# Attention's matmuls as four 64x64 products at a time, and the values of two groups over two steps

## Chip, cores and metric

The kernel runs on one core of one Trainium2 chip, in one launch. The metric is the device time of that launch in microseconds; lower is better.

## What is computed

The input is 8 images of 512 channels by 32x32 pixels (N = 1024 pixels), all in float32. Two attention blocks follow each other. Cut to what matters here:

```python
# layer 0: group norm, 8 heads of 64 channels, projection, group norm, residual
hn  = group_norm(x, gn1_scale, gn1_bias)
qkv = einsum('bchw,oc->bohw', hn, w_qkv) + b_qkv          # 1x1 convolution
q, k, v = split(qkv.reshape(b * 8, 3 * 64, n), 3, axis=1)
wgt = softmax(einsum('bct,bcs->bts', q * 64**-0.25, k * 64**-0.25))
a   = einsum('bts,bcs->bct', wgt, v)
x   = x + group_norm(einsum('bchw,oc->bohw', a, w_proj) + b_proj, gn2_scale, gn2_bias)
# layer 1: one head of 512 channels with weight norm and RMS norm
qkv = einsum('oc,bcn->bon', weight_norm(v_qkv, g_qkv), x)
qkv = qkv / (rms(qkv) + 1e-4)
h   = einsum('bij,bcj->bci', softmax(q^T k * 512**-0.5), v)
x   = (x + einsum('oc,bcn->bon', weight_norm(v_out, g_out), h)) * 2**-0.5
```

The change concerns layer 0's attention: the projections of q and k, the scores (q times k) and the values (softmax times v).

## The kernel before

**Order.** Every engine call goes through `InOrder` (line 26), which pins it to the order in which the Python code makes it. What an engine does next is therefore written out by hand, and each engine works its list strictly in that order. A float32 matmul of the program stands in the trace as two MATMULs and two LDWEIGHTS (weight loads), two passes over the same tile.

**Layer 0's attention.** For each image `b`, the loop at line 1414 runs 32 steps (`STEPS`). A step `i = 8j + r` treats 128 query pixels (block `r` of 8) of a pair of heads (`j` of 4): the pair's 128 channels lie on the 128 partitions, one head on each half. `Heads.step` (line 635) issues in this order:

1. `softmax(i)`, line 573: for each of the two heads DVE takes the negated row maximum of the scores (`nm<-s`, 128x1024) and ACT the exponential with the row sum (`p<-s,nm`).
2. `values(g)`, line 610, where it is due: TensorE multiplies v by the transposed softmax `pT` of a group `g` of two steps (`RG` = 2, so 256 query pixels). There are 8 blocks of 128 key pixels and 2 heads; a matmul has 128 rows, 64 columns and 256 moving columns. The two heads' results go to the two partition halves of one PSUM bank (`po`), so two matmuls run beside each other on the two column halves of the array. ACT then adds a bias and writes `a`.
3. `fill`: a piece of a projection, where it is due.
4. `scores(i + 1)`, line 558: four matmuls of 64 rows (one head's channels), 128 columns and 512 moving columns, two at a time on the two row halves of the array, into two PSUM tiles `s` of two banks each. There are three such tiles (`ps_s`, line 102).
5. `turn()`, line 585: DVE transposes step `i - 1`'s softmax in 32x32 blocks (`pb<-p`), and SP issues four DMAs of 256 KB (`pT<-pb`) that bring it into `pT` with the key pixels on the partitions.
6. `scale()`, line 603: DVE's reciprocal of the row sums, and GpSimd (POOL) multiplies step `i`'s softmax by it.
7. `later`: GpSimd additions that a projection left over, among others.

`values(g)` comes in steps 5, 7, 9 and so on (`LAG` = 5 and `RG` = 2, lines 367 to 370); the last row of group `g` was turned in step `2g + 2`, so the step of use is the third after it. A projection piece comes in nearly every other step (`projects`, line 1421). Groups 14 and 15 come after the loop.

**Projections.** For the first image, and for each image's first pair of heads, `project_rows` (line 398) makes q and k in four pieces. A piece is 8 matmuls of 64x128 with 512 moving columns: the two row halves of the channels run beside each other into two banks, which ACT copies out and GpSimd adds. For the other pairs, `project_seven` (line 476) makes q and k from seven products instead of eight. Its first piece (n = 0) is one product of 128x128 with two terms into one bank; pieces 1 to 3 are two 64x128 products beside each other, with four terms each. At the first step of pairs 1 and 2 the short first piece is filled up with the first two key blocks of a group's values (line 1434; `values` with `most` = 2).

**Buffers.** `ps_m` (line 103) has two PSUM banks of 128x512 floats, given out in turn by `bank()` to projections and values alike. `prob` and `block`, for `p` and `pb`, have two buffers each. `pT` is taken from seven large tiles (`Slots`, line 37) that it shares with the images and v; a group's tile is given back once its values are done.

**Around it.** After an image's 32 steps come layer 0's output projection and layer 1, both made of 128x128 matmuls, with the next image's v between them. In steps 0 to 2 of the next image the last products of layer 1 (128x128) are still part of `fill`.

Of the kernel before, what the change touches and what calls it, by code (L numbers as in the profile page):

```python
# [13 lines left out]
P = 128  # L14
# [38 lines left out]
def attention_blocks_kernel(  # L53
# [133 lines left out]
    for g in range(P // SQ):  # L187
        VE.tensor_copy(same[:, g * SQ : (g + 1) * SQ], flat)
    VE.tensor_scalar_mul(same2, same, 2.0 ** 0.5)
    shift = const.tile([P, 1], F32, name="shift")  # L190
    VE.memset(shift, -16.0)
    cols = const.tile([P, NCOLS], F32, name="cols")
# [283 lines left out]
    def project_seven(b, j, right, made):  # L476

        w, tmp = near["qk7"][:, (j - 1) % 2], [near["v#"][:, k * HN : (k + 1) * HN] for k in range(3)]  # L480

        def turned(t):
            return t.rearrange("p (m be) -> p be m", be=4)

        def add(to, a, b_):
            return lambda: PO.tensor_add(to, a, b_)

        def pieces():
            pm = bank(f"pq7_{b}_{j}_0")
# [8 lines left out]
            adds = (  # L498
                ([], []),
                ([], []),  # L500
                ([add(q2, q2, q1), add(k2, k2, turned(q2))], [add(k1, k1, k2), add(k2, k2, turned(tmp[1]))]),
                ([add(q1, q1, tmp[0]), add(q2, q2, tmp[1])], [add(q2, q2, tmp[2])]),
            )
            for n in range(1, 4):
                pms = [bank(f"pq7_{b}_{j}_{n}_{r}") for r in range(2)]
                for k in range(CI):
                    for r in range(2):
                        PE.matmul(pms[r], w[halves[r], CI * n - 2 + k, :], right(r, n, k), start=(k == 0), stop=(k == CI - 1))
                if n == 1:
                    AC.activation(q1, pms[0], AF.Identity, bias=bqs[:, j : j + 1])  # L510
                    AC.copy(k1, turned(pms[1]))
                elif n == 2:
# [39 lines left out]
    class Heads:  # L552
        def __init__(self, b, hn, v, qk):
            self.b, self.hn, self.v, self.a = b, hn, v, None
            self.qk = {0: qk}
            self.pT, self.ps, self.waiting, self.open = {}, None, None, None

        def scores(self, i):
            j, r = divmod(i, NB)
            qk = self.qk[j]  # L560
            self.ps = [ps_s.tile([P, N], F32, tag="sc", name=f"s0_{self.b}_{i}_{hh}") for hh in range(2)]
            for c in range(2):
                cs = slice(c * HN, (c + 1) * HN)
                for hh in range(2):
                    PE.matmul(
                        self.ps[hh][:, cs],
                        qk[halves[hh], 0, r * P : (r + 1) * P],
                        qk[halves[hh], 1, cs],
                        start=True,
                        stop=True,  # L570
                    )

        def softmax(self, i):
            p = prob.tile([P, 4, 2, N // 4], F32, tag="p", name=f"p0_{self.b}_{i}")
# [35 lines left out]
        def values(self, g, most=NT):  # L610

            j, t0 = g // (NB // RG), g % (NB // RG) * TG
            po, s0 = self.open or (bank(f"po0_{self.b}_{g}", TG), 0)
            s1 = min(s0 + most, NT)
            self.open = (po, s1) if s1 < NT else None
            if self.a is None:
                self.a = big(f"a_{self.b}")
            for s in range(s0, s1):
                for hh in range(2):
                    ch = (2 * j + hh) * D  # L620
                    PE.matmul(
                        po[halves[hh], :],
                        self.v[:, s, ch : ch + D],
                        self.pT[g][:, :, :, hh, s, :],
                        start=(s == 0),
                        stop=(s == NT - 1),
                    )
            if self.open:
                return
# [3 lines left out]
            del self.pT[g]  # L633

        def step(self, i, fill=(), early=(), later=()):
# [12 lines left out]
            self.scale()  # L648
            for f in later:
                f()  # L650
# [763 lines left out]
    for b in range(B):  # L1414
        hn, more = heads.hn, b + 1 < B
        todo, due, rest = iter(()), [], []
        for i in range(STEPS):
            j, r = divmod(i, NB)
            due = rest

            projects = (i - LAG) % RG if not b or i not in (2, 3) else i == 3

            def project():
                nonlocal due, rest
# [27 lines left out]
            if not b:  # L1452


                if i == CI:
                    hn_next = big(f"hn_{b + 1}")
                    norm1 = Norm1(b + 1, hn_next)
                if 0 <= i - CI < CI:
                    later.append(lambda: load_x(b + 1, hn_next, i - CI))
                if 0 <= i - CI - 2 < 2 * CI:  # L1460
                    later.append(lambda: norm1.stats((i - CI - 2) // 2, i % 2))
                k = i - 3 * CI - 2
                if k == 0:
                    coeffs = norm1.gn.all_steps()
                    early += [norm1.aggregate, lambda: next(coeffs)]
                elif 0 < k < 8:
                    early.append(lambda: next(coeffs, None))
                if 0 <= k - 7 < CI // 2:
                    for ci in range(2):
                        later.append(lambda ci=ci: norm1.apply(2 * (k - 7) + ci, PO))  # L1470

            if b and j == 1 and r < 7:
                fetch_qk(CI - 1, b, slice(2 * r, 2 * r + 2))
# [143 lines left out]
```

## Time and profile before

| | |
|---|---|
| median of 3 runs | 3155.25 us (3152.35 to 3157.02) |
| the profiled execution's own time | 3153.42 us |
| its span in the profile | 3151.6 us |
| PE (matmul) busy | 3122.2 us, 99%, 13014 MATMULs |
| DVE / ACT / POOL busy | 75% / 34% / 45% |
| granted TensorE clock | 0.998 |
| DMA | 451.58 MB, mean 143 GB/s |

The profile is one execution, taken by the hardware. A row of the costliest groups reads: line, engine, operation, output tile, input tiles, shape (for matmuls: rows*columns of the array that are used, then partitions x moving columns), count, then the busy time of the group and the mean duration of one. Nearly all calls stand under line 34, the helper of `InOrder`, so groups are told apart by their tiles: `s` scores, `po` values, `pq` and `pqk` the projections by `project_seven` and `project_rows`. A timeline row gives the start, the time from the first start to the last end, and how many equal instructions were merged into it. Matmuls overlap in the pipeline, so the pitch of two is read from their starts and not from their durations.

### The profile page before, as it was taken

How to read it: one execution, taken by the hardware profiler on the slowest of the kernel's cores; microseconds unless marked ns; L12 is line 12 of the kernel's file. 1: busy time of each engine (PE TensorE's matmuls, PEld its weight loads, DVE VectorE, ACT ScalarE, POOL GpSimd, SP SyncE). 2: the span in 40 equal slices, each digit the busy share in tenths (PEclk: the TensorE clock that was granted, in tenths of full speed). 3: DMA queues.
4: the chain of work that ended last, by engine and by line, in shares of the span. 5: the costliest groups of instructions: out<-in, count | busy, mean ns of one | idle time of the engine just before them, and what ended most of it. 6: DMA issues, size and time to landing. Idle time of an engine off the chain costs nothing.

```text
span 3151.6 us, 36676 instructions
## 1 busy us (share of the span) xinstructions
PE 3122.2 (99%) x13014; PEld 1603.9 (51%) x13014; DVE 2366.5 (75%) x3213; ACT 1070.7 (34%) x1844; POOL 1409.9 (45%) x1129
## 2 busy tenths in 40 slices
PE   9999999999999999999999999999999999999899
PEld 5445554456444554445544555445554455444454
DVE  5697777867788767886679876797677877778765
ACT  2353133521245212551125502354123531245311
POOL 1555235732367314771247703566235642356114
PEclk9999999999999999999999999999999999999999
DMA  6788225862268512784128832388224872158600
GB/s 207 198 210 236 77 57 136 223 203 76 64 173 225 184 58 62 206 229 159 47 77 223 228 120 54 110 223 223 94 72 117 217 232 77 30 147 221 199 7 34
DMA packets 213950, 451.58 MB, mean 143 GB/s; under 512 B 23652, under 2 KB 42760, under 8 KB 208008
## 3 DMA queue, kind: packets, MB, share of 16 engines
q1 hardware_dynamic: 213648, 449.21, 50.3%
q8 instruction: 104, 1.70, 0.2%
q14 instruction: 78, 0.64, 0.1%
q10 hardware_dynamic: 120, 0.02, 0.0%
HBM read 137.26 MB, written 29.56 MB: 53 GB/s over the span
## 4 chain that ended last, share of the span: by engine, by line
PE 89%; DMA 3%; DVE 3%; POOL 2%; SPq 2%; issue 1%; ACT 0%; DVEq 0%; ACTq 0%; POOLq 0%
PE s L34 13%; PE po L34 12%; PE p L34 7%; PE pq L34 7%; PE p_v_T L34 6%; PE p_v_B L34 5%; PE py L34 4%; PE pqk L34 4%; PE p_u_T L34 4%; PE pa L34 4%; PE pe_e L34 3%; PE pe_bc L34 3%; PE pe_a L34 3%; PE p_o_T L34 3%; PE p_u_B L34 3%; PE p_o_B L34 2%
## 5 line engine op out<-in xcount | busy, mean ns | idle before, releaser
L34 ACT ACTIVATE p<-s,nm 128x1024 f32<-128x1024 f32 x512 | 565.6, 1109 | 794.1 <-DVE nm L34 510.2
L34 POOL TENSOR_SCALAR p<-p,tt 128x1024 f32<-128x1024 f32 x512 | 566.0, 1118 | 410.7 <-DVE tt L34 393.0
L34 DVE TENSOR_REDUCE nm<-s 128x1 f32<-128x1024 f32 x512 | 602.8, 1219 | 150.1 <-PE s L34 149.3
L34 DVE STREAM_TRANSPOSE pb<-p 128x2048 f32<-128x2048 f32 x256 | 589.9, 2304 | 37.6 <-POOL p L34 18.4
L34 PE MATMUL s<-qk 64*128 64x512 f32 x2048 | 501.5, 605 | 3.8 <-ACT p L34 2.1
L34 PE MATMUL po<-pT,v 128*64 128x256 f32 x4096 | 473.4, 383 | 1.1 <-issue 1.1
L34 PEld LDWEIGHTS po<-pT,v 128*64 128x64 f32 x4096 | 282.3, 137 | 227.9 <-issue 28.2
L34 PEld LDWEIGHTS s<-qk 64*128 64x128 f32 x2048 | 187.8, 186 | 245.7 <-issue 219.3
L34 PE MATMUL p<-e,v 128*128 128x512 f32 (+1 forms) x520 | 228.2, 590 | 2.5 <-DVE x L34 2.5
L34 POOL TENSOR_TENSOR x<-x,o 128x1024 f32<-128x1024 f32 x21 | 52.1, 2515 | 348.8 <-ACT o L34 348.8
L34 POOL TENSOR_TENSOR esum<-esum,e 128x512 f32<-128x512 f32 x96 | 141.7, 1500 | 148.4 <-ACT e L34 148.4
L34 POOL TENSOR_TENSOR u<-u,xy 128x512 f32<-128x512 f32 x64 | 79.2, 1269 | 278.0 <-DMA xy<-far_rinv 205.4
L34 PE MATMUL pq<-hn,qk 64*128 64x512 f32 (+1 forms) x420 | 191.8, 593 | 0.0
L34 ACT ACTIVATE e<-e,shift,rinv 128x512 f32<-128x512 f32 x96 | 75.8, 810 | 268.8 <-DVE e L34 268.8
L34 DVE TENSOR_TENSOR v<-v,p_v_T 128x256 f32<-128x256 f32 x300 | 114.3, 417 | 69.0 <-PE p_v_T L34 50.0
L34 PEld LDWEIGHTS p<-e,v 128*128 128x128 f32 x520 | 97.0, 190 | 130.1 <-issue 121.3
L34 PE MATMUL pqk<-hn,qk 64*128 64x512 f32 (+1 forms) x672 | 158.2, 590 | 0.0
L34 PE MATMUL pq<-t,qk 64*128 64x512 f32 x336 | 151.0, 589 | 0.0
L34 PE MATMUL pq<-v,qk 64*128 64x512 f32 x336 | 150.9, 589 | 0.0
L34 POOL TENSOR_TENSOR esum<-e 128x512 f32<-128x512 f32 x16 | 25.1, 1585 | 274.3 <-ACT e L34 274.3
L34 PE MATMUL py<-x,gram 128*128 128x512 f32 x320 | 140.6, 599 | 4.4 <-DVE x L34 4.4
L34 POOL TENSOR_TENSOR qk<-qk,v 128x512 f32<-128x512 f32 x96 | 127.2, 1335 | 3.2 <-ACT v L34 1.6
(240 smaller groups left out, 4738.1 us busy)
## 6 DMA issues: line engine op xcount, KB each, us to landing
pT<-pb SPq DMA_DIRECT2D x1024, 256.0 KB, 4.5
hn<-in_x_dram SPq DMA_DIRECT2D x32, 512.0 KB, 5.8
x<-in_x_dram SPq DMA_DIRECT2D x32, 512.0 KB, 6.9
out_dram<-x SPq DMA_DIRECT2D x63, 256.0 KB, 2.0
score<-far_score SPq DMA_DIRECT2D x8, 1792.0 KB, 7.0
value<-far_value SPq DMA_DIRECT2D x8, 1792.0 KB
v<-far_v SPq DMA_DIRECT2D x49, 256.0 KB, 4.6
proj<-far_proj SPq DMA_DIRECT2D x7, 1792.0 KB
```

What stands on the lines that cost most here:

```text
L34: return lambda *args, **kw: self._pin(call(*args, **kw))
```

## The change

All matmuls of `scores`, `project_rows` and `project_seven` become 64x64: a helper `quads` splits the 128 output columns of each into two halves, so that four matmuls, one in each quarter of the array, form a unit. The two row halves still go to two banks.

The values of two groups, `g` and `g + 1`, are made together over two consecutive steps, as 64x64 matmuls too. In the first step the upper row half (64 of each block's 128 key pixels) works for `g` in one bank and the lower half for `g + 1` in another. In the second step (`second` = 1) the halves change banks, and each bank gets the rest of its sum. Between the two, ACT copies one column of each bank into a small tile `begun`. Each bank is copied out once, at the end.

In `project_seven`, the product n = 0 is split between the first two pieces: each of them holds half of the columns of n = 1 (four terms) and half of n = 0 (two terms), both with 256 moving columns. ACT copies out four halves instead of whole banks, and GpSimd adds the row halves of n = 0.

The order changes with it. `LAG` becomes 6; values come in steps 6, 7, 10, 11, and so on to 30, 31, projection pieces in the two steps between them (8, 9, 12, 13, ...); in steps 0 to 5 they come at 0, 3, 4, 5 (for the first image 0, 2, 4, 5). The extra `values(..., 2)` at the first step of a pair is gone. The norm of the second image moves by a few steps. Groups 14 and 15 keep the old form.

```diff
-    STEPS, LAG = CI * NB, 5
+    STEPS, LAG = CI * NB, 6
+    def quads(outs, left, right, first=True, last=True):
+        for out_, l, r in zip(outs, left, right):
+            for cs in halves:
+                PE.matmul(out_[cs], l[:, cs], r, start=first, stop=last)
...
 # project_rows
                     for ci in range(CI):
-                        for r in range(2):
-                            PE.matmul(
-                                pms[r],
-                                w[halves[r], ci, :],
-                                hn[halves[r], ci, hs],
-                                start=(ci == 0),
-                                stop=(ci == CI - 1),
-                            )
+                        quads(pms, [w[rs, ci, :] for rs in halves], [hn[rs, ci, hs] for rs in halves], ci == 0, ci == CI - 1)
...
 # project_seven
-            pm = bank(f"pq7_{b}_{j}_0")
-            run(matmuls(pm, [(w[:, k, :], right(None, 0, k)) for k in range(2)]))
-            AC.copy(tmp[1], pm)
-            yield [], []
...
+            low, high = slice(0, TG), slice(TG, HN)
+            for n, cols in enumerate((low, high)):
                 pms = [bank(f"pq7_{b}_{j}_{n}_{r}") for r in range(2)]
+                product(pms, 1, cols, low)
+                product(pms, 0, cols, high)
+                AC.activation(q1[:, cols], pms[0][:, low], AF.Identity, bias=bqs[:, j : j + 1])
+                AC.copy(tmp[1][:, cols], pms[0][:, high])
+                AC.copy(k1[:, :, n * D : (n + 1) * D], turned(pms[1][:, low]))
+                AC.copy(q2[:, cols], pms[1][:, high])
+                yield [add(tmp[1][:, cols], tmp[1][:, cols], q2[:, cols])], []
+            for n in range(2, 4):
+                pms = [bank(f"pq7_{b}_{j}_{n}_{r}") for r in range(2)]
+                product(pms, n, slice(0, HN), slice(0, HN))
...
 # scores
-                for hh in range(2):
-                    PE.matmul(
-                        self.ps[hh][:, cs],
-                        qk[halves[hh], 0, r * P : (r + 1) * P],
-                        qk[halves[hh], 1, cs],
-                        start=True,
-                        stop=True,
-                    )
+                quads(
+                    [ps[:, cs] for ps in self.ps],
+                    [qk[rs, 0, r * P : (r + 1) * P] for rs in halves],
+                    [qk[rs, 1, cs] for rs in halves],
+                )
...
+        def values_two(self, g, second):
+            if not second:
+                self.pos = [bank(f"po0_{self.b}_{g + k}", TG) for k in range(2)]
+            for s in range(NT):
+                for r, rs in enumerate(halves):
+                    k = r ^ second
+                    for hh in range(2):
+                        PE.matmul(
+                            self.pos[k][halves[hh], :], self.v[rs, s, self.channels(g, hh)], self.pT[g + k][rs, :, :, hh, s, :],
+                            start=not second and s == 0, stop=s == NT - 1, skip_group_check=bool(second),
+                        )
+            for k in range(2):
+                if not second:
+                    AC.copy(begun[:, k : k + 1], self.pos[k][:, :1])
+                else:
+                    self.out(g + k, self.pos[k])
...
 # step
-            if i >= LAG and (i - LAG) % RG == 0:
-                self.values((i - LAG) // RG)
+            if i >= LAG and (i - LAG) % (2 * RG) < 2:
+                self.values_two((i - LAG) // (2 * RG) * 2, (i - LAG) % 2)
...
 # loop over the steps
-            projects = (i - LAG) % RG if not b or i not in (2, 3) else i == 3
+            projects = i in (0, 3 if b else 2, 4, 5) if i < NB else (i - LAG) % (2 * RG) > 1
...
-            if b and r == 0 and 0 < j < CI - 1:
-                fill.append(lambda: heads.values((i + 1 - LAG) // RG, 2))
```

More of the change, by code (lines that the diff above doesn't have):

```diff
@@ L189, in attention_blocks_kernel @@
     VE.tensor_scalar_mul(same2, same, 2.0 ** 0.5)
+    begun = const.tile([P, 2], F32, name="begun")
     shift = const.tile([P, 1], F32, name="shift")
@@ L497, in pieces @@
             k1, k2 = (kp[:, :, th * P : (th + 1) * P] for th in range(2))
[L498 to L502, printed above, removed]
-            )
-            for n in range(1, 4):
-                pms = [bank(f"pq7_{b}_{j}_{n}_{r}") for r in range(2)]
[L506 to L512, printed above, removed]
+            adds = {
+                2: ([add(q2, q2, q1), add(k2, k2, turned(q2))], [add(k1, k1, k2), add(k2, k2, turned(tmp[1]))]),
+                3: ([add(q1, q1, tmp[0]), add(q2, q2, tmp[1])], [add(q2, q2, tmp[2])]),
+            }
@@ new lines, in product @@
+            def product(pms, n, cols, to):
+                count = CI if n else 2
+                for k in range(count):
+                    quads(
+                        [pm[:, to] for pm in pms],
+                        [w[rs, max(CI * n - 2, 0) + k, :] for rs in halves],
+                        [(right(r, n, k) if n else right(None, 0, k)[rs])[:, cols] for r, rs in enumerate(halves)],
+                        k == 0,
+                        k == count - 1,
+                    )
+            low, high = slice(0, TG), slice(TG, HN)
@@ L514, in pieces @@
+            for n in range(2, 4):
+                pms = [bank(f"pq7_{b}_{j}_{n}_{r}") for r in range(2)]
+                product(pms, n, slice(0, HN), slice(0, HN))
+                if n == 2:
                     AC.copy(q2, pms[0])
@@ L555, in __init__ @@
             self.qk = {0: qk}
-            self.pT, self.ps, self.waiting, self.open = {}, None, None, None
+            self.pT, self.ps, self.waiting = {}, None, None
         def scores(self, i):
@@ L563, in scores @@
                 cs = slice(c * HN, (c + 1) * HN)
-                for hh in range(2):
-                    PE.matmul(
-                        self.ps[hh][:, cs],
-                        qk[halves[hh], 0, r * P : (r + 1) * P],
-                        qk[halves[hh], 1, cs],
-                        start=True,
-                        stop=True,
-                    )
+                quads(
+                    [ps[:, cs] for ps in self.ps],
+                    [qk[rs, 0, r * P : (r + 1) * P] for rs in halves],
+                    [qk[rs, 1, cs] for rs in halves],
+                )
         def softmax(self, i):
@@ L608, in scale, with out @@
             self.waiting = (i, p)
-        def values(self, g, most=NT):
+        def out(self, g, po):
             j, t0 = g // (NB // RG), g % (NB // RG) * TG
-            po, s0 = self.open or (bank(f"po0_{self.b}_{g}", TG), 0)
-            s1 = min(s0 + most, NT)
-            self.open = (po, s1) if s1 < NT else None
             if self.a is None:
                 self.a = big(f"a_{self.b}")
[L618 to L629, printed above, removed]
             AC.activation(self.a[:, j, t0 : t0 + TG], po, AF.Identity, bias=col(BV, j))
@@ L633, in values, with channels @@
             del self.pT[g]
+        def channels(self, g, hh):
+            ch = (2 * (g // (NB // RG)) + hh) * D
+            return slice(ch, ch + D)
+        def values(self, g):
+            po = bank(f"po0_{self.b}_{g}", TG)
+            for s in range(NT):
+                for hh in range(2):
+                    PE.matmul(
+                        po[halves[hh], :], self.v[:, s, self.channels(g, hh)], self.pT[g][:, :, :, hh, s, :],
+                        start=(s == 0), stop=(s == NT - 1),
+                    )
+            self.out(g, po)
+        def values_two(self, g, second):
+            if not second:
+                self.pos = [bank(f"po0_{self.b}_{g + k}", TG) for k in range(2)]
+            for s in range(NT):
+                for r, rs in enumerate(halves):
+                    k = r ^ second
+                    for hh in range(2):
+                        PE.matmul(
+                            self.pos[k][halves[hh], :], self.v[rs, s, self.channels(g, hh)], self.pT[g + k][rs, :, :, hh, s, :],
+                            start=not second and s == 0, stop=s == NT - 1, skip_group_check=bool(second),
+                        )
+            for k in range(2):
[3 more added lines that the diff above has]
+                    self.out(g + k, self.pos[k])
         def step(self, i, fill=(), early=(), later=()):
             self.softmax(i)
-            if i >= LAG and (i - LAG) % RG == 0:
-                self.values((i - LAG) // RG)
+            if i >= LAG and (i - LAG) % (2 * RG) < 2:
+                self.values_two((i - LAG) // (2 * RG) * 2, (i - LAG) % 2)
             for f in fill:
@@ L1461, in attention_blocks_kernel @@
                     later.append(lambda: norm1.stats((i - CI - 2) // 2, i % 2))
-                k = i - 3 * CI - 2
+                k = i - 4 * CI
                 if k == 0:
                     coeffs = norm1.gn.all_steps()
[L1465 to L1468, printed above, removed]
+                    early.append(norm1.aggregate)
+                if 0 <= k < 6:
+                    early += [lambda: next(coeffs, None)] * (2 if k < 2 else 1)
+                if 0 <= k - 6 < CI // 2:
                     for ci in range(2):
-                        later.append(lambda ci=ci: norm1.apply(2 * (k - 7) + ci, PO))
+                        later.append(lambda ci=ci: norm1.apply(2 * (k - 6) + ci, PO))
             if b and j == 1 and r < 7:
```

## The prediction

> **What bounds the kernel now.** The page comes first: TensorE is busy for 99% of the span, so a gain has to come out of its time.
>
> ```profile
> span 3151.6 us, 36676 instructions
> PE 3122.2 (99%) x13014; PEld 1603.9 (51%) x13014; DVE 2366.5 (75%) x3213; ACT 1070.7 (34%) x1844; POOL 1409.9 (45%) x1129
> L34 PE MATMUL s<-qk 64*128 64x512 f32 x2048 | 501.5, 605 | 3.8 <-ACT p L34 2.1
> L34 PE MATMUL po<-pT,v 128*64 128x256 f32 x4096 | 473.4, 383 | 1.1 <-issue 1.1
> L34 PEld LDWEIGHTS po<-pT,v 128*64 128x64 f32 x4096 | 282.3, 137 | 227.9 <-issue 28.2
> ```
>
> Scores and values together waited 5 us in the whole run. Busy is not the same as streaming, however. The timeline of PE alone, in the second image's attention, shows what lies between:
>
> ```profile
> 622.80 3.60 PE L34 MATMUL pqk<-hn,qk 64*128 64x512 f32 x16
> 626.23 1.88 PE L34 MATMUL s<-qk 64*128 64x512 f32 x8
> ...
> 604.89 1.88 PE L34 MATMUL s<-qk 64*128 64x512 f32 x8
> 606.70 3.67 PE L34 MATMUL po<-pT,v 128*64 128x256 f32 x32
> 610.31 1.99 PE L34 MATMUL s<-qk 64*128 64x512 f32 x8
> ...
> 615.56 1.88 PE L34 MATMUL s<-qk 64*128 64x512 f32 x8
> ```
>
> Eight pairs of pqk take 626.23 - 622.80 = 3.43 us: 429 ns for a pair with 512 columns, and a single 128x128 matmul has the same pitch. With 256 columns it is 216 ns. From 604.89 to 615.56 two steps pass in 10.67 us. They hold 8 pairs of s (3.43), 16 of po (3.45) and 8 of pq (3.43), together 10.32. The other 0.35 us is the change of shape from 64x128 to 128x64 (0.15) and back (0.20).
>
> The third reading is the softmax's way to the values, which the change shortens in steps: DVE's timeline, SP's timeline, and the tile view of pT.
>
> ```profile
> 606.80 2.36 DVE L34 TENSOR_REDUCE nm<-s 128x1 f32<-128x1024 f32 x2 [0.53 <-PE s L34]
> 609.08 2.30 DVE L34 STREAM_TRANSPOSE pb<-p 128x2048 f32<-128x2048 f32 x1
> ...
> 606.26 2.49 SPq L34 DMA_DIRECT2D pT<-pb  x3
> 608.79 1.33 SPq L34 DMA_DIRECT2D pT<-pb  x1
> ...
> DMA to landing us min/median/max: 3.5/4.5/6.4
> ```
>
> I count time from the start of a step's first reduction, which comes 0.2 us after the end of its scores on PE (615.56 + 1.72 = 617.28, reduction at 617.48). The transposition ends at 4.58 (606.80 to 611.38). The four DMAs are issued after it, the last one about 2.6 us later (608.79, after a transposition that ended at 606.23), and each lands about 4.5 us after its issue. So the last quarter of pT is there 2.6 + 4.5 = 7.1 us after the transposition. The semaphores of all 256 turns give a median of 7.2 and 6.3 as the shortest; for the rows that now matter most (every fourth step), the landing is at 11.8 in a step's own time. Before, a group was used three steps after the turn, at about 15.8: four microseconds to spare, and no wait in the page.
>
> **The change, part by part.**
>
> *Streaming: nothing.* The multiplications are the same. Counted in passes: before, 1848 pairs and 84 single matmuls of 512 columns; after, 1680 fours of 512 and 504 fours of 256 columns: 829 us each way. Values: 2048 pairs before; 1792 fours and 256 pairs after. This assumes that a four has the pitch of a pair. No row shows a four. Row halves run beside each other (s) and column halves too (po), and a four is both at once. The bounds are no loss, and twice the pitch: 1680 x 0.429 + 2296 x 0.216 = 1217 us. I take no loss, since each half of it is in the trace.
>
> *Weight loads and issue.* 21554 matmuls and as many loads instead of 13014. A four with 256 columns needs 8 instructions in 216 ns, 27 ns each. The densest stretch of the trace, after a wait at 193.83 us, passed 65 instructions of PE's queue in 1445 ns, 22 ns each. So it fits, but barely; cost 0. Loads of po (137 ns) start 2 ns after a matmul on the same rows and run under it. The Trainium skill ("TensorE: Matmul & The Clock Gate", Part 3, what overlaps) says that a load overlaps with matmuls in flight only where the row group differs; by that rule each of 3976 fours would wait 137 ns, an estimate of 545 us. The po row, same row group, contradicts it: PEld's 282 us lie inside PE's time.
>
> *Changes of shape: -45 us.* Counted in the order in which the two programs stand, 366 changes before and 110 after. At half of 0.35 us, 256 x 0.176 = 45 us. Between layer 1's 128x128 and s the trace has 0.20 each way; for 64x64 I take the same.
>
> *Values of two groups: the new wait.* Let P1, P2, V1, V2 be the four steps of the new cycle. V1 uses groups g and g + 1. The last row of g + 1 belongs to the V2 before, and is turned in P1. So the use is two steps after the turn instead of three. PE reaches V1 at 2 x 5.16 - 0.2 = 10.1 (a step without changes of shape: 1.72 + 3.44 = 5.16). The last DMA lands at 11.8. The matmuls of g + 1 stand third in the list, PE's queue waits in order, and behind them are all other values of V1, the next scores, and through them DVE and ACT. The trace has one place where po waited for pT, the last group of the last image: its transposition ended at 2954.91, PE came at 2961.92 and po began at 2963.02:
>
> ```profile
> 2957.51 0.72 SPq L34 DMA_DIRECT2D pT<-pb  x1
> 2963.02 3.24 PE L34 MATMUL po<-pT,v 128*64 128x256 f32 x28 [1.10 <-issue]
> ```
>
> That is 8.1 us after the transposition, with the last landing at 2962.60, and 0.4 more for the semaphore instructions ahead of the matmul. I add 0.35 to 11.8: V1 starts at 12.1, 2.0 us late. Bounds: 6.6 (shortest such landing) + 0.1 gives 11.3, and 8.1 gives 12.7.
>
> From there the cycle is one chain: 12.1, V1 3.45, s 1.72, V2 3.45, s 1.72, 0.2 to the next reduction: 22.7 us. Its length does not depend on P1 and P2 as long as the two together take less than 12.
>
> *Short pieces.* Pieces 0 and 1 of project_seven hold 8 passes of n = 1 and 4 of n = 0 at 0.216, 2.59 us, a step of 4.31. DVE needs 4.66 (the shortest steps of before), and the banks that ACT must empty come about 0.6 us late for piece 1: ACT reaches them at about 3.5, after both exponentials, and four half copies take 1.1. For pairs 1 and 2 all of this lies ahead of V1 and is covered by its wait; without that wait it would cost about 1 us for each of 14 pairs (two in each of seven images), 14 us.
>
> *At no cost:* the two copies into begun (nearest row: 0.47 us for 256 columns; V2 is 1.72 us of scores away, ACT is 34% busy); 42 half additions on POOL (45% busy); pT's slots, which are reused at once, but V2 ends at 3.25 and the DMA into the slot is issued at 4.58; SP's queue keeps its order.
>
> **The sum.** From the first reduction of step 4 to that of step 31, before: 144.8, 142.2, 141.6, 141.6, 141.6, 142.7, 143.0, 144.0 us in the eight images, 1141.3 in all. After: six cycles and 12.1 + 3.45 + 1.72 + 0.2 = 17.5, so 153.7 each, 1229.6: +88. Steps 0 and 3 of seven images: the first piece has 2.59 us instead of 1.72 (+0.87), and step 3 falls from 5.15 to DVE's 4.66 (-0.49): 0.4 each, +3. Together +91, and 3153.4 + 91 = 3245. Cross-check: -45, 56 waits of 2.0 (+112), 14 shorter pairs of steps ahead of V1 (+24): +91. The medians lie 1.8 above the profiled run: 3246.
>
> **Rivals.**
> - *pT is there in time (faster).* One thing decides it: if the landing in P1 comes 2.0 us sooner, 5.2 after the transposition, V1 does not wait, and the time is 3155 - 45 + 14 = 3124. The break-even is at about 5.6. For it: DMA traffic in a cycle is thinner. Against: none of 256 turns landed before 6.3, not even those with an idle queue ahead of them, since issue and flight alone make 7.1. Chance 0.06.
> - *Fours run two at a time.* Then 1217 is added, steps become 8.6 us long and the wait for pT disappears: 3155 - 45 + 1217 = 4327. For it: no row of four. Chance 0.07.
> - *Fours run, but each 256-column one is held by issue or loads.* Each 27 ns more costs 2296 x 0.027 = 62 us of PE time, in V1 and V2 on the chain: some 3300 to 3400. Chance 0.07.
>
> **How the numbers follow.** The forecast has 0.80. Its own uncertainty is the landing, 0.5 us either way on 56 waits: 28 us. The range reaches up to part of the third rival and down to a landing 1 us sooner: 3190 to 3315. Faster 0.06, within 0.2% (6 us, about what a measurement here can tell) 0.01, slower 0.93.
>
> **What would show it.** Right: in PE's waits, po waits for the DMA pT<-pb about 56 times for some 2 us, more at pairs 1 and 2; first reductions of every fourth step 22.7 us apart; s and po at pitches of 429 and 216 ns for four; few waits elsewhere. The steps P, P, V between would stay near 5.16. Wrong: if the waits of po add up to less than 45 us, if V1 starts at 10.1 after P1's reduction, or if fours have a longer pitch than pairs.

## The result, and the profile after

| | before | after |
|---|---|---|
| median | 3155.93 us (3152.35 to 3157.02) | 3258.47 us (3254.08 to 3262.3) |
| ratio | | 1.0328, 95% interval 1.0315 to 1.0341 |
| profiled execution, its span | 3153.42 us, 3151.6 us | 3262.3 us, 3260.3 us |
| granted TensorE clock | 0.998 | 0.99 |

The change makes the kernel 3.3% slower. The profiled execution after is the slowest of its four (3254.08 to 3262.3), so what is counted in it below is rather high for the median. The page shows as much work as before, and a PE that no longer covers the span:

```profile
span 3260.3 us, 54073 instructions
PE 3139.2 (96%) x21554; PEld 1732.9 (53%) x21554; DVE 2365.2 (73%) x3213; ACT 1104.7 (34%) x2061; POOL 1439.7 (44%) x1171
```

Among the costliest groups, values now carry an idle time of 89.4 us where they had 1.1, and scores still carry none:

```profile
L34 PE MATMUL s<-qk 64*64 64x512 f32 x4096 | 580.9, 591 | 0.7 <-ACT p L34 0.7
L34 PE MATMUL po<-pT,v 64*64 64x256 f32 (+1 forms) x7680 | 548.4, 393 | 89.4 <-DMA pT<-pb 42.5 <-DMA qk<-far_qk 21.0 <-ACT p L34 9.4
```

The list of PE's waits (total us, times, longest) gives that idle time several names:

```profile
PE po L34 <- DMA pT<-pb: 42.5, 28, 3.7
PE po L34 <- DMA qk<-far_qk: 21.0, 9, 3.0
PE po L34 <- ACT p L34: 9.4, 3, 3.4
PE po L34 <- DMA v<-far_v: 8.4, 6, 1.8
PE pq L34 <- DVE v L34: 6.2, 7, 0.9
```

The rows of po are one wait; the row of pq is another, taken up at e7_piece_at_2. A wait is put down to the latest event that the trace sees before it ends, and other transfers land at about the same time. Taken one by one, 53 of the 56 first value steps (V1) stop for 0.29 to 3.85 us after their first matmuls (counted from the end of the last one's pitch), and all of these restart 0.09 to 0.45 us after the last landing of pT's four DMAs; the other three wait less than 0.2 us. One of them on three timelines (PE, DVE, SP), in the fifth image's step 14:

```profile
1768.44 0.60 PE L34 MATMUL po<-pT,v 64*64 64x256 f32 x4
1770.22 3.46 PE L34 MATMUL po<-pT,v 64*64 64x256 f32 x58 [1.19 <-issue]
1773.31 0.60 PE L34 MATMUL s<-qk 64*64 64x512 f32 x2
1773.48 0.41 PE L34 MATMUL po<-pT,v 64*64 64x256 f32 x2
```

```profile
1758.35 2.36 DVE L34 TENSOR_REDUCE nm<-s 128x1 f32<-128x1024 f32 x2 [0.55 <-PE s L34]
1760.63 2.30 DVE L34 STREAM_TRANSPOSE pb<-p 128x2048 f32<-128x2048 f32 x1
```

```profile
1762.95 3.63 SPq L34 DMA_DIRECT2D pT<-pb  x4
```

P1's first reduction is at 1758.35, its transposition ends 4.58 later, and V1 goes on at 1770.22, 11.87 after the reduction (prediction: 12.1). V1 itself takes 3.46 us, so fours do run four at a time at a pair's pitch. The third and fourth PE rows show something else: the first scores (upper row half) start before the last values (lower row half) are done. The upper half got four matmuls through before the wait and keeps that lead of two 216 ns passes. The next reduction reads the upper half's scores and so comes 0.4 us sooner than the prediction's chain has it. A cycle like this one is 21.9 us long, not 22.7; the mean of all 48 is 22.90.

What the prediction did not have stands in the windows of one V1 in the third image (columns: stretch, its length, PE busy with the count of matmuls, granted clock, DMA share, GB/s):

```profile
955.10:958.50 3.40, 1.05 (x11) 1.00 0.83 233
959.20:962.60 3.40, 3.40 (x39) 0.50 0.85 257
962.70:966.10 3.40, 3.40 (x56) 1.00 0.86 224
```

```profile
958.50 5.14 PE L34 MATMUL po<-pT,v 64*64 64x256 f32 x58 [2.35 <-DMA qk<-far_qk]
```

PE stood still for 2.35 us by this row, and soon after its restart the granted clock fell to half for 3.41 us: this V1 takes 5.14 us instead of 3.46. It happens 13 times in attention (11 times for 3.41 us, twice for 6.83: 51.2 us, so at most 25.6 us lost), and never in the attention of before.

From the first reduction of step 4 to that of step 31 the eight images now take 1236.2 us (before 1141.3): +94.8. Steps 0 to 3 take 28.61 us in seven images instead of 26.94 (step 0 alone 9.21 instead of 7.27), and 1.3 less in the first image: +10.4. The rest of the span changes by 3.5.

### The profile page after: what moved, and what is told of

It is laid out like the page before. It is cut to its first block, busy times and chain, and to the rows that moved or that the text cites. A ratio compares the mean times of both kernels' runs of the same rounds, so it can differ in the third digit from the quotient of the medians.

```text
span 3260.3 us, 54073 instructions
## 1 busy us (share of the span) xinstructions
PE 3139.2 (96%) x21554; PEld 1732.9 (53%) x21554; DVE 2365.2 (73%) x3213; ACT 1104.7 (34%) x2061; POOL 1439.7 (44%) x1171
## 2 busy tenths in 40 slices
DMA packets 214018, 452.68 MB, mean 139 GB/s; under 512 B 23652, under 2 KB 42760, under 8 KB 208008
## 4 chain that ended last, share of the span: by engine, by line
PE 63%; POOL 10%; DVE 8%; DMA 8%; issue 7%; SPq 3%; ACT 1%; DVEq 0%; POOLq 0%; ACTq 0%
PE po L34 10%; PE p_v_T L34 6%; DVE pb L34 5%; PE s L34 5%; PE p_v_B L34 5%; POOL p L34 5%; DMA pT<-pb 4%; PE py L34 4%; POOL qk L34 4%; PE p_u_T L34 3%; PE pe_bc L34 3%; PE pe_e L34 3%; PE pe_a L34 3%; SPq L34 3%; PE p_o_T L34 3%
## 5 line engine op out<-in xcount | busy, mean ns | idle before, releaser
L34 PE MATMUL po<-pT,v 64*64 64x256 f32 (+1 forms) x7680 | 548.4, 393 | 89.4 <-DMA pT<-pb 42.5
L34 PE MATMUL s<-qk 64*64 64x512 f32 x4096 | 580.9, 591 | 0.7 <-ACT p L34 0.7
L34 PEld LDWEIGHTS po<-pT,v 64*64 64x64 f32 (+1 forms) x7680 | 394.3, 139 | 241.1 <-issue 117.7
L34 PEld LDWEIGHTS s<-qk 64*64 64x64 f32 x4096 | 225.1, 133 | 206.3 <-issue 179.2
L34 PE MATMUL pq<-hn,qk 64*64 64x256 f32 (+1 forms) x1680 | 210.9, 421 | 0.0
L34 POOL TENSOR_TENSOR esum<-esum,e 128x512 f32<-128x512 f32 x96 | 141.6, 1500 | 148.4 <-ACT e L34 148.4
L34 PE MATMUL pqk<-hn,qk 64*64 64x512 f32 (+1 forms) x1312 | 173.9, 590 | 1.0 <-POOL hn L34 0.9
L34 PE MATMUL pq<-t,qk 64*64 64x256 f32 (+1 forms) x1008 | 157.0, 450 | 6.2 <-DVE v L34 6.2
L34 PE MATMUL pq<-v,qk 64*64 64x512 f32 x672 | 151.9, 590 | 0.0
L34 PEld LDWEIGHTS pq<-hn,qk 64*64 64x64 f32 x1680 | 105.7, 133 | 56.5 <-issue 32.3
```

What stands on the lines that cost most here:

```text
L34: return lambda *args, **kw: self._pin(call(*args, **kw))
```

## Experiments

All times are medians; the median of before beside them was between 3154.7 and 3156.1 us.

**e1_landed_tile: the wait taken away.**

```diff
-  self.pT[g + k][rs, :, :, hh, s, :]
+  self.pT[g + (k if second else 0)][rs, :, :, hh, s, :]
```

> The changed kernel, but the first of two value steps multiplies with group g's pT for both banks, so it reads no tile that was turned in the step but one before it (the first half of g + 1's sum is left out, and half of g's is made twice; the number, shape and order of all instructions is the same). Theory (the loss is the wait for the last DMA of pT, and what that wait does to the clock): po's idle time of 89 us goes, the 13 stretches at half clock (51 us long, up to 26 us lost) go with it, and what the shorter steps ahead cost without the cover comes back, some 14 us: 3130 to 3160 us. Rival (a four of 64x64 with 256 columns is held by its loads or its issue, and the wait only covers it): the time stays above 3230 us.

Measured: 3169.7 us, ratio to before 1.0044 (1.0033 to 1.0055). PE's waits for pT go to 1.1 us, and one half-clock stretch is left in attention. So the wait, with what hangs on it, was worth 89 us. But the time is 10 us above the top of the expected range, and the change without its wait is still slower than before: step 4 to 31 takes 1141.2 us, as if nothing had been gained. DVE's transposition tells where the gain went, with this kernel's row first and the next experiment's below it:

```profile
L34 DVE STREAM_TRANSPOSE pb<-p 128x2048 f32<-128x2048 f32 x256 | 590.8, 2308 | 106.0 <-POOL p L34 67.0 <-DMA pT<-pb 26.9 <-POOL v L34 1.7
```

```profile
L34 DVE STREAM_TRANSPOSE pb<-p 128x2048 f32<-128x2048 f32 x256 | 590.2, 2305 | 46.0 <-DMA pT<-pb 22.8 <-POOL p L34 18.6 <-DVE nm L34 0.5
```

**e5_no_adds: the same, without project_seven's whole additions.**

```diff
-                yield adds[n]
+                yield [], []
```

> The kernel of e1_landed_tile, and besides it leaves out the seven whole additions with which project_seven ends each pair on POOL (the two half additions stay). Without the wait the 27 steps from step 4 to 31 of the eight images took 1141.2 us there, as before the change, and not the 45 us less that fewer changes of shape should give; its trace shows the transposition waiting 67 us for POOL's scaling of p. Theory (seven additions of 1.35 us in two neighbouring steps stand in POOL's queue ahead of the scaling, and that takes the gain): those 67 us and scores' waits for p fall to near nothing, and the time is 3125 to 3150 us. Rival (the gain was never there: fours with 256 columns, or DVE, hold the steps): 3160 to 3172 us as in e1_landed_tile.

Measured: 3133.9 us, 0.9935 (0.9920 to 0.9950). The theory holds: 36 us sat in POOL's queue. The kernel before makes the same additions, and there its transposition waits no longer than here without them:

```profile
DVE pb L34 <- POOL p L34: 18.4, 12, 2.3
```

POOL's timeline in e1_landed_tile, with DVE's below it, shows how:

```profile
914.55 1.29 POOL L34 TENSOR_TENSOR qk<-qk 128x512 f32<-128x512 f32 x1
915.92 4.02 POOL L34 TENSOR_TENSOR qk<-qk,v 128x512 f32<-128x512 f32 x3
919.89 2.24 POOL L34 TENSOR_SCALAR p<-p,tt 128x1024 f32<-128x1024 f32 x2
```

```profile
916.86 0.12 DVE L34 RECIPROCAL tt<-tt 128x2 f32<-128x2 f32 x1
916.90 2.33 DVE L34 TENSOR_REDUCE nm<-s 128x1 f32<-128x1024 f32 x2
922.16 2.31 DVE L34 STREAM_TRANSPOSE pb<-p 128x2048 f32<-128x2048 f32 x1 [2.93 <-POOL p L34]
```

The sums were ready at 916.98, but the scaling of p started at 919.89, behind four additions, and the transposition came 2.93 us late. Pieces 2 and 3, which bring these additions, used to stand two steps apart; now they are neighbours. From step 4 to 31 undisturbed images take 137.2 us here and 141.6 before, 4.4 less each, and all eight take 1107.7 instead of 1141.3. In these stretches PE waits 1.0 us in all here and 2.0 before, so the difference lies in PE's own work and not in the additions left out. What differs there is the shape of the matmuls: apart from the setup, the trace before has 366 changes of shape, this one 110.

**e4_before_fours: the fours alone, in the kernel before.**

```diff
-  for hh in range(2): PE.matmul(self.ps[hh][:, cs], qk[halves[hh], 0, ...], qk[halves[hh], 1, cs], ...)
+  quads([ps[:, cs] for ps in self.ps], [qk[rs, 0, ...] for rs in halves], [qk[rs, 1, cs] for rs in halves])
   # likewise in project_rows and in pieces 1 to 3 of project_seven
```

> The kernel before with one part of the change: scores and the row pieces of both projections are made of four 64x64 matmuls instead of two 64x128; values, their order, the waits and all else stay as before. Theory (a four has the pitch of a pair, and the values' change of shape stays): 3150 to 3165 us. Rival (a four costs more than a pair by its issue or loads): with 1680 fours of 512 columns each 27 ns more would be 45 us, 3200 us.

Measured: 3152.2 us, 0.9987 (0.9977 to 0.9996). Fours of 512 columns cost nothing: twice as many instructions and loads for scores and projections do not show. The trace still has the 366 changes of shape, and little is gained.

**e2_two_queues: all four DMAs issued at once.**

```diff
-                SY.dma_start(
+                (SY if q in (0, 1) else AC).dma_start(
```

> The changed kernel, with two of the four DMAs of a turn issued by ACT instead of SP; nothing else differs. Theory (the spacing of the issues on one queue sets the landing): the last issue comes about 0.8 us after the transposition instead of 2.6, the last landing at 5.3 to 6.0 instead of 7.1, V1 waits at most half a microsecond, the granted clock never falls in attention, and the time is 3130 to 3180 us. Rival (the flights share the DMA engines, so that earlier issue only lengthens them): the landing stays at 6.5 to 7.1 and the time above 3220 us.

Measured: 3302.7 us, 1.0461 (1.0443 to 1.0479): the theory is wrong, and the kernel 44 us slower. The issues did move. In the median of all turns of steps 5 to 31 the last one comes 0.67 us after the transposition instead of 2.31. But its flight grows from 4.70 to 6.04 us, and the last landing is at 7.30 instead of 7.08. At the turns that V1 waits for it is 7.40 on average (7.05 in the changed kernel), and the latest 10.35 (8.68). The flights by the DMA issues, in the changed kernel and here:

```profile
pT<-pb SPq DMA_DIRECT2D x1024, 256.0 KB, 4.3
```

```profile
pT<-pb ACTq DMA_DIRECT2D x512, 256.0 KB, 5.9
pT<-pb SPq DMA_DIRECT2D x512, 256.0 KB, 5.1
```

Later landings of these turns explain only part of the 44 us: 15.2 come from steps 4 to 31, 16.7 lie between an image's last step and the next image's first (2.4 in each of seven), and 10.2 after the last step of all. There the last turn of an image lands 12.5 to 15.3 us after its transposition (changed kernel: 6.6 to 7.3); in the last image PE waits 8.6 us ahead of the group that needs it, in the changed kernel 0.5. Why this one turn is so late was not followed.

**e11_half_bytes: half the bytes.**

```diff
-  out=self.pT[g][:, r, q].rearrange("p hh B j -> p (hh B j)"), in_=pb[32 * q : 32 * q + 32].rearrange(...)
+  out=self.pT[g][:, r, q, 0].rearrange("p B j -> p (B j)"), in_=pb[32 * q : 32 * q + 32, :, 0]
   # values read pT[...][..., 0, s, :] for both heads
```

> The changed kernel with half the bytes in each of a turn's DMAs: only the first head's half of the transposed softmax is moved, and the values of both heads are made from it (the second head's values are therefore another result; number and shape of all instructions stay). Theory (the four transfers of 1 MB share a rate, so that bytes and not issue or a fixed delay set the last landing): it falls from 7.1 to 4 to 5.2 us after the transposition, V1 hardly waits, half-clock stretches go, and the time is 3160 to 3185 us, as in e1_landed_tile. Rival (issue on the queue and a fixed flight, as the prediction put it, 2.6 + 4.5): the landing stays at 6.5 to 7.1 and the time above 3230 us.

Measured: 3161.3 us, 1.0019 (1.0010 to 1.0029). The flight falls to 2.6 us and the last landing to 4.63 after the transposition, with the issues where they were or a little sooner (the last at 1.92). The number of DMA packets is the same, 214018, so it is the bytes that differ.

```profile
pT<-pb SPq DMA_DIRECT2D x1024, 128.0 KB, 2.6
```

Together with e2_two_queues this says that a turn's 1 MB is held by what the transfers can move, not by the queue that issues them: 7.1 to 7.3 us for 1 MB with late issues or early ones, 4.6 for half of it. V1 hardly waits any more (all values 6.3 us), and the change is still not faster than before.

**e3_filler and e6_half_filler: work put into the wait.**

```diff
+  for s in range(4):                       # e6_half_filler: range(2)
+      for r, rs in enumerate(halves):
+          for hh in range(2):
+              PE.matmul(self.pos[r][halves[hh], :], self.v[rs, s, ...], self.pT[g][rs, :, :, hh, s, :], start=..., stop=...)
```

> The changed kernel with 16 more matmuls of po's shape (0.86 us of PE at 216 ns for a four) on group g ahead of each first value step; their sums are written over, the result is the same. Theory (PE stands idle there for pT, and a shorter pause keeps the clock up): the extra work disappears in the wait, fewer than the 13 stretches at half clock are left, and the time is 3230 to 3260 us, not above the changed kernel's. Rival (PE's work is the bound): 56 x 0.86 = 48 us more, 3306 us.

> The kernel of e3_filler with half the extra work. (A matmul of the program is two passes: e3_filler's 16 were 32 MATMULs, eight fours, 1.73 us for each first value step and not 0.86, 97 us of PE time in all; this kernel's 8 are 0.86 us and 48 us in all.) Theory (the landing sets when V1 starts, and a pause under about 2.4 us leaves the clock up): the work is hidden in the wait and the half-clock stretches stay away, so full cycles take 21.9 us instead of e3_filler's 22.37 and the time is 3225 to 3245 us, below both the changed kernel and e3_filler. Rival (PE's work counts): 48 us over the changed kernel, 3306; or e3_filler's 3248 is a floor that something else sets, and this is 3248 too.

Measured: 3248.0 us (1.0289, 1.0272 to 1.0306) and 3243.9 us (1.0284, 1.0269 to 1.0300). In e3_filler 97 us of extra PE work (1.73 us for each V1; the first expectation had counted half of it) made the kernel 10 us faster than the changed one, and no half-clock stretch is left in attention. With half the filler, 48 us of work, it is 14.5 us faster than the changed kernel, with two such stretches. Neither could happen if PE's work set V1's start. The ratios of the two fillers cannot be told apart, though the second was expected to be faster; in the traces it is as expected, with cycles of 21.9 us. In e3_filler many cycles last exactly 22.37 us, which is PE's own work (the 20.64 of undisturbed cycles in e5_no_adds, and 1.73): there the filler, not the landing, is the bound. The idle time of values shrinks with it, here in e3_filler:

```profile
L34 PE MATMUL po<-pT,v 64*64 64x256 f32 x9472 | 614.0, 377 | 14.2 <-DMA pT<-pb 7.3 <-DMA qk<-far_qk 4.3 <-issue 2.1
```

**e8_g_first: useful work put into the wait.**

```diff
+  if not second:      # g alone, then both, then g + 1 alone
+      order = [(s, 0) for s in range(4)] + [(s + 4 * (1 - r), r) for s in range(4) for r in range(2)] + [(s + 4, 1) for s in range(4)]
```

> The changed kernel with the matmuls of each first value step in another order: four key blocks of group g alone (two at a time, 1.73 us), then four blocks of both groups (four at a time, 1.73 us), then the other four blocks of g + 1 (1.73 us). The same matmuls, and only g + 1 waits for the late tile. Theory (only the tile of g + 1 is late, and the pause throws the clock): PE works through the wait, V1 still ends at about 15.3 us after P1's first reduction in full cycles, the half-clock stretches go, and the time is 3225 to 3250 us. Rival (both tiles are late, or fours are not the reason that V1 takes 3.45 us): each V1 ends 1.73 us later, 3258 + 97 = 3355 us.

Measured: 3238.6 us, 1.0265 (1.0250 to 1.0281). V1 takes 1.73 us longer and ends when it did; values idle 21.7 us instead of 89.4, four half-clock stretches are left instead of 13. Nine stretches fewer are 11 periods of 3.41 us, at half speed 18.8 us; the gain is 19.8. So of the 89 us some 20 are the clock, and some 70 the late tile itself. The split is an estimate, as the stretches are counted in one execution of each kernel.

**e7_piece_at_2: step 0 relieved.**

```diff
-  projects = i in (0, 3 if b else 2, 4, 5) if i < NB else ...
+  projects = i in ((2, 3, 4, 5) if b else (0, 2, 4, 5)) if i < NB else ...
```

> The changed kernel with the first piece of project_seven in step 2 instead of step 0 for the second to the last image. In the changed kernel's trace step 0 takes 9.21 us (before: 7.27), and PE waits 0.9 us there for DVE's sums to empty a bank, as the piece now needs both banks of ps_m. Theory: that wait goes, steps 0 to 3 fall by 1.0 to 1.7 us in each of seven images, 3246 to 3252 us. Rival (step 0 is long because of its work, which only moves to step 2, or the sums of step 2 hold the bank in the same way): 3256 to 3262 us.

Measured: 3251.6 us, 1.0312 (1.0295 to 1.0329). Steps 0 to 3 take 28.40 us instead of 28.61: the rival was right. Step 2 is now 9.41 us long, and the wait has gone with the piece:

```profile
PE pq L34 <- DVE v L34: 7.6, 7, 1.1
```

The last products of layer 1 use a bank in step 2 as in step 0, and a piece that needs both has to wait for DVE to empty it. The median is 7 us below the changed kernel's, within the range of the theory, but the intervals of the two ratios overlap, and only 1.5 us are from here; the profiled execution had nine half-clock stretches instead of 13.

**e9_old_order_fours and e10_sums_later: the fours in the old order.** The row halves of a group's values go to two banks, ACT copies both out and POOL adds them, 0.73 us a group. e9 is the kernel of e4_before_fours with

```diff
+  def values_four(self, g):
+      pos = [bank(...) for r in range(2)]
+      for s in range(NT):
+          for r, rs in enumerate(halves):
+              for hh in range(2):
+                  PE.matmul(pos[r][halves[hh], :], self.v[rs, s, ...], self.pT[g][rs, :, :, hh, s, :], start=(s == 0), stop=(s == NT - 1))
+      AC.activation(to, pos[0], AF.Identity, bias=col(BV, j))
+      AC.copy(rest, pos[1])
+      self.sums.append(lambda: PO.tensor_add(to, to, rest))   # run after scale()
-  fill.append(lambda: heads.values((i + 1 - LAG) // RG, 2))
   # project_seven of pairs 2 and 3 as in the changed kernel
```

> The order of the kernel before (a group's values in one step, the third after its turn; projections in the steps between; the additions on POOL spread as before), but everything in attention's steps of 64x64: scores and projections as in the changed kernel (pair 1 keeps the old project_seven, so that the first piece of step 0 needs one bank), and a group's values as fours whose row halves go to two banks; ACT copies out both, and POOL adds them, 0.73 us for each of 112 groups (1 us as a bound). The filling up with two key blocks at pairs 1 and 2 is left out; the last two groups of an image keep the old values. Theory (the changes of shape are worth 40 us, and the changed kernel loses them and more to the late pT, the clock and POOL's burst, none of which is here): each value step falls from 5.52 to about 5.2 us, the pairs without filling lose up to 0.5 us each, and the time is 3110 to 3135 us, below before. Rival (both banks must now be empty for each step, so that PE waits for ACT's copies where before one bank was free): 112 waits of 0.3 to 0.6 us give the 40 us back, 3145 to 3175 us.

Measured: 3160.9 us, 1.0013 (1.0005 to 1.0022): a miss. Its first image takes 155.7 us from step 4 to 31 (before: 144.8), for a reason that no side had named. PE has to wait until DVE has read the norm's means out of a bank that values now need:

```profile
197.76 6.03 PE L34 MATMUL po<-pT,v 64*64 64x256 f32 x58 [3.98 <-DVE mean L34]
```

So e10:

```diff
-                self.values_four((i - LAG) // RG)
+                (self.values_four if self.b else self.values)((i - LAG) // RG)
...
+            if i % NB in (1, 2, 3) or i + 3 > STEPS:   # the sums run here only
```

> The kernel of e9_old_order_fours with two edits that its trace asked for. In its first image two steps took 12.9 and 12.1 us: with both banks taken by values, PE's next step waited until DVE had read the norm's means out of one; the first image takes the old values back. And scores of a new pair waited 9.1 us (10 times) for POOL's additions to q and k, behind the new additions of value halves; these now run in the second to fourth step of a pair only. Theory (these two are what kept the gain of fewer changes of shape away): the first image falls by 11 to 14 us, the other waits by 5 to 10, and the time is 3135 to 3148 us, below before. Rival (steps 4 to 8 of each image, where the transposition waits for pb and SP's queue, take the rest whatever POOL does): only the first image's part comes, 3146 to 3155 us, no clear difference from before.

Measured: 3142.8 us, 0.9963 (0.9950 to 0.9975). This version is 0.4% faster than the kernel before, a small gain but clear of the noise, and 116 us faster than the changed one. The wait of scores for q and k falls from 9.1 to 4.6 us, values wait 1.5 us in all, and PE is back at 99%, with POOL busier than in either kernel:

```profile
PE 3104.6 (99%) x20686; PEld 1621.0 (52%) x20686; DVE 2366.4 (75%) x3213; ACT 1104.8 (35%) x2012; POOL 1499.9 (48%) x1255
```

That POOL does more here and holds nobody up much (the transposition waits 29.8 us for its scaling, in e1_landed_tile 67.0) says that it matters where the additions stand, not only how many there are. The trace has 135 changes of shape instead of 366. Step 4 to 31 falls by 20 us against before (1121.3); of that, the end of the last image gives 8 back, where the output projection waits 3.2 us for the last addition.

## Why the prediction was right, point by point

3246 was predicted, 3258 measured, and the mechanism is the predicted one: V1 waits for the last DMA of pT, and the wait sets the length of the cycle. Its terms fared differently.

- **Streaming 0, issue and loads 0:** right (V1 in 3.46 us for 16 fours of 256 columns; e4_before_fours for 512).
- **Changes of shape, -45:** the direction is shown by e5_no_adds and e10_sums_later; 4.4 us in an undisturbed image of e5_no_adds, where the term and the short pieces together would give 3.6.
- **The start of V1, 12.1 us after P1's first reduction:** 12.07 on average. The transposition ends at 4.74 (4.58 put in), the last landing comes 7.05 later (7.2), the restart 0.27 after it (0.35). The 56 waits add up to 98 us (112).
- **From there to the next cycle, 10.6:** 10.39 in the 35 cycles without a half-clock stretch, as the upper row half's lead makes the next reduction come sooner, and 12.03 in the 13 with one. The mean cycle is 22.90 instead of 22.7.
- **The clock was left out.** The prediction let PE wait 2 us 56 times and took its speed after each wait as given. By the two means above the clock cost 13 x 1.64 = 21 us (about 20 by e8_g_first, at most 25.6 by the length of the stretches). The lead of the upper half, which the prediction did not have either, gave some 10 back. So +94.8 from step 4 to 31 is near the predicted +88.3 partly by luck: two terms that were missing have opposite signs.
- **Steps 0 to 3, +0.4 each, were +1.67.** The prediction counted PE's passes (+0.87 for the first piece) and not that the piece now needs two banks while layer 1's last sums still hold one. In total +10.4 instead of +3.
- **"At no cost", POOL:** mis-sized where it was looked at and missed beside it. The half additions are harmless, but the order also makes pieces 2 and 3 neighbours, and their whole additions then cost 36 us. In the changed kernel most of this is hidden by the wait for pT, as the prediction said of all that lies ahead of V1.
- **Where the 7.1 us come from:** "issue and flight alone make 7.1" named the sum rightly and its parts wrongly. 2.6 and 4.5 are not two prices: take the issue away and the flight grows.
- **The rival "pT is there in time"** was priced at 3124, with break-even at a landing of 5.6 us. With the landing at 4.63 the time is 3161, and with no wait at all 3170: the rival's condition would not have made the change faster. Missing in its price were POOL's 36 us and some 7 in steps 0 to 3.

From before to after, the ledger by runs reads: 3155, then -21 for the change without the wait for pT and without the whole additions (e5_no_adds, 3134: -34 from step 4 to 31 with fewer changes of shape, +10 in steps 0 to 3, the rest small), +36 for the additions (e1_landed_tile, 3170), +69 for the late tile (e8_g_first, 3239), +20 mainly for the clock (3258). The order of the entries matters, since the wait covers part of what stands above it.

## What to carry to other kernels

When a use moves a step nearer to its producer, time the whole way, and price each wait on TensorE with the clock that it costs as well as its length. When an order is rewritten, list for every engine's queue which work becomes neighbours, not only how much work it has: an engine at 45% can still make others late. And a gain that a new wait swallows can often be had without the wait: here fours in the old order, with POOL's additions moved out of the way, were 0.4% faster than the kernel before (e10_sums_later).

## What the runs showed of the hardware

- **Short waits cost the clock.** In the changed kernel (waits counted from the end of the last matmul's pitch to the restart) no wait of V1 up to 2.2 us was followed by a half-clock stretch, six of the ten between 2.4 and 2.8 us were, and all seven from 2.83 us on. In e2_two_queues three came after 1.78 to 1.90 us. The stretches are 3.41 us long or a multiple of it, and those of a run start on one grid of 3.41 us. The Trainium skill ("TensorE: Matmul & The Clock Gate", Part 1, on the clock gate) describes windows of 3413 ns that run freely and a clock that is either half or full: these runs agree in both. Its table puts the cold state after at least one idle window of about 3.4 us; here waits of 2.4 to 2.8 us were enough, and the measurement decides.
- **The grid tells which waits counted.** The share of a window in which PE streamed is an estimate from the starts of its matmuls, with 429 ns for 512 columns and 216 for 256. In the changed kernel's attention PE streamed for less than 42% of each of the 13 windows just ahead of a stretch, and for more than 42% of each of the 466 others that ran at full clock. In e7_piece_at_2 nine windows of up to 33% were followed by half clock, and none of the others, from 46% on. So a wait of 2.5 us counted when most of it fell into one window. The border is not sharp everywhere: in the other runs windows of 39 to 53% went both ways, and in e8_g_first, where V1 begins and ends with half of the array, two of 65 and 70% were followed by half clock. No run varied the place of a wait by itself.
- **A turn's 1 MB lands 7.1 us after the transposition from one queue and 7.3 from two** (medians): 256 KB flights take 3.6 us as the first of a turn on one queue, 4.7 as the last of four, 6.0 as the last on two queues; 128 KB flights take 2.5 to 2.7 as the first and the last.
- **One row half of the array ran ahead of the other.** After a wait that held only the lower row half, the upper one stayed 0.43 us ahead: its first scores began at 1773.31, and the last values of the lower half, which stand earlier in the program, at 1773.48.
